# First pass of a two-layer attention kernel: query and output products as seven products of halves, formed inside one strip

## The chip, the cores and the metric

The kernel runs on one core of a Trainium2 chip. The metric is the device time of one execution in microseconds. Of the kernel before, three executions took 3718.24, 3722.89 and 3724.72 us; the median is 3722.89 us. The engines are named as in the profile: PE (TensorE: matrix products; PEld is its weight load), DVE (VectorE), ACT (ScalarE), POOL (GpSimd), SP (SyncE, which here issues the DMAs). Each engine works through its own queue in order. A product lands in one of eight PSUM banks, of 512 float32 columns each, from which DVE or ACT must read it.

## The reference, cut to what matters

The input has 8 images of 256 channels and 64x64 positions, all float32. Layer 0 is an attention with keys and values from a 4x4-strided convolution; layer 1 is a linear attention with a depthwise convolution.

```python
xr = layernorm(conv(x, w_sr, stride 4))              # 16x16 = 256 positions
q  = w_q @ x                                         # 256x256 by 256x4096
k, v = split(w_kv @ xr)
attn = softmax(q_head.T @ k_head * 32**-0.5)         # 8 heads of 32, 256 keys
out  = w_out @ (attn @ v)
x2   = x + gamma_s * out                             # end of layer 0
qkv  = w_qkv @ x2                                    # 768x256 by 256x4096, layer 1
...                                                  # depthwise, linear attention, projection
```

The change touches `w_q @ x`, `gamma_s * (w_out @ ...)` and how the seven products of `w_qkv @ x2` are put together.

## The kernel before, in words

The kernel has three passes. Only the first, the function `first_pass`, is touched. It computes layer 0 and the product `w_qkv @ x2`, and stores `x2`, the q and k planes, k and v to scratch memory for the later passes.

**Tiling.** An image's 4096 positions are cut into 8 strips of 512 columns (`QB`). `strips(b, s)` is a strip in SBUF: 128 partitions, two channel halves, 512 columns. The list `order` runs over image `b`, strip `s` and channel half `c`: 8 x 8 x 2 = 128 iterations, counted by `n`. Each iteration handles four heads of one strip.

**One iteration `n` of the main loop (from L1045), as it stands on PE.**

1. `scores(..., 0, q)` (L795): four products of 32 rows for the keys 0 to 127, side by side in four row groups, into four banks. ACT then turns each bank into `e` (L801, an exponential).
2. `valued` and `counted` for the iteration before: eight products into one bank `av` (L819) and four into one bank `den` (L839). `den` takes the sums `ej` that POOL adds from the two sets of `e` (`joined`, L832).
3. `scores(..., 1, q)`: the same for the keys 128 to 255, with four more `e`.
4. `copied` and `normed` for the iteration before: ACT copies `av` to `att` (L843). DVE turns `den` over (L852), takes the reciprocal (L854), turns it back (L856) and multiplies `att` (L858).
5. Some of the products of `qkv` (L917), the query products of the next iteration, and, in every second iteration, the output products `added`. Where the next image's keys are in preparation (`keys_values`), products `sr` (L707) of 256 columns are put in between: 64 for each image but the first.

`queries` (L780) makes one channel half of a strip's queries as two products of 512 columns; ACT copies the bank (L788). `added` (L873) does the same for the output, and DVE multiplies the bank by `gamma_s` and adds it into the strip in one instruction (L874), after which the strip is stored.

**Seven products.** `qkv` works on a pair of strips (a group `g`) and a pair of output halves. The operand is a 2x2 arrangement of blocks, channel half by strip, and so is the weight. Instead of eight products of a 128x128 weight with 512 columns it makes seven: products 1 to 7 of sums and differences of blocks, whose results DVE adds up (`part`, `whole`, `stage`: L930, L933, L986, L990, L999). Every product has a bank of its own. The differences of strips come from `differences`: three DVE instructions and one on POOL (L888 to L891). The sums of weights come from `combine_weights`. The pairs 1, 2, 0 of a group are spread over four iterations in portions of 7, 4, 7 and 3 products. Of the results, `turned` transposes (L937) and the `stage` copies on ACT (L943) come one iteration later (`late`, run by `catch_up`).

**Banks.** `bank` hands out eight banks in rotation; a bank named as kept (`av`, `den`, `sr`) leaves the rotation until `given_back`. A product waits until the readers of the bank's previous content are done.

**Order.** The program's instructions are put in order for each engine, ahead of time, by a planner with its own estimates of cost; instructions marked with `keep_in_program_order` stay behind all that the program wrote earlier for that engine. In the kernel before, few are marked (the transposes L852 and L937, the weight products of `conv_weights`); PE's order is the planner's.

`conv_weights` (L683) makes 64 blocks of weights for the second pass on DVE, one in each iteration from 17 to 80.

Of the kernel before, what the change touches and what calls it, by code (L numbers as in the profile page):

```python
# [574 lines left out]
def first_pass(ctx: ExitStack, tc: tile.TileContext, a, fine, planes, x2d, kd, vd, wtd):  # L575
# [30 lines left out]

    consts, x_tiles = {}, {}
# [33 lines left out]
    combined = halves.tile([P, 3, 4, P], F32, tag="combined", name="combined")  # L641

    def combine_weights():
        w = consts["wqkv"].rearrange("p c (j r o) -> p c j r o", j=3, r=2)
        a11, a12, a21, a22 = (w[:, c, :, r] for r in range(2) for c in range(2))
        s1, s2, s3, s4 = (combined[:, :, i] for i in range(4))
        nc.vector.tensor_add(s1, a21, a22)
        nc.vector.tensor_sub(s2, s1, a11)
        nc.vector.tensor_sub(s3, a11, a21)
        nc.vector.tensor_sub(s4, a12, s2)  # L650
# [23 lines left out]
    def conv_weights():  # L674
        for j in (2, 3, 0, 1):
            wd = made.tile([P, 16, 6, 16], F32, tag="wd", name=f"wd_{j}", bufs=1)
            nc.sync.dma_start(wd[:, :, :4], a.w_big[:, j].rearrange("p g (n f) -> p g n f", n=4))

            tc.keep_in_program_order(nc.vector.tensor_add(wd[:, :, 4:], wd[:, :, 0:4:2], wd[:, :, 1:4:2]))
            for g in range(16):  # L680
                w = made.tile([P, 6 * 16, D1], F32, tag="wb", name=f"wb_{j}_{g}", bufs=1)
                tc.keep_in_program_order(
                    nc.vector.tensor_tensor(  # L683
                        w,
                        wd[:, g].rearrange("p n f -> p (n f)").unsqueeze(2).to_broadcast([P, 6 * 16, D1]),
                        consts["wsmall"][:, j, g].unsqueeze(1).to_broadcast([P, 6 * 16, D1]),
                        ALU.mult,
                    )
                )
                nc.sync.dma_start(wtd[j][:, g], w.rearrange("p n o -> p (n o)"))  # L690
                yield
# [4 lines left out]
    def keys_values(b):  # L696
# [5 lines left out]
        for f, tap in taps:  # L702
            w = keys.tile([P, 2, C], F32, tag="wsr", name=f"wsr_{b}_{f}", bufs=3)
            nc.sync.dma_start(w, a.w_sr[:, :, tap])
            for ci in range(2):
                for oc in range(2):
                    nc.tensor.matmul(  # L707
# [13 lines left out]
        for ci in range(2):  # L721
            nc.tensor.matmul(mean, mean_w, xr[:, ci], start=(ci == 0), stop=(ci == 1))
# [7 lines left out]
        for kc in range(2):  # L730
            for ci in range(2):
                nc.tensor.matmul(
# [311 lines left out]
    for n in range(n_all + 6):  # L1044
# [28 lines left out]
        for f in products[:3]:  # L1073
            f()
# [795 lines left out]
```

## Time and profile before

| what | value |
|---|---|
| median of three executions | 3722.89 us |
| the profiled execution: its time, its span | 3723.3 us, 3721.5 us |
| granted PE clock, mean | 0.991 |
| PE busy | 3655.3 us (98%) |
| DVE busy | 2050.1 us (55%) |
| ACT busy | 1348.7 us (36%) |
| POOL busy | 1362.7 us (37%) |
| first score product to last `qkv` product | 57.5 us to 1976.4 us |

The page cuts the span into 40 slices of 93 us. PE shows 9 tenths or more in nearly all of them. The first 21 slices are the first pass; the DMA queues are about half busy there and nearly full in the second pass. All times "at" are microseconds from the span's start. In the timeline a row gives the start, the length from the first start to the last end, the engine, the line, the operation, what is written and read, the shape, and how many equal instructions follow each other; in brackets stands the idle time of the engine before it and what ended it. A float32 product shows as two PE records.

### The profile page before, as it was taken

The page shows a single profiled execution, that of the slowest core. Times are in us where ns is not written, and L with a number is a line of the kernel's source. Part 1 is how long each engine was busy: PE and PEld are TensorE (multiplying, and loading weights), DVE is VectorE, ACT ScalarE, POOL GpSimd, SP SyncE. Part 2 cuts the span into 40 slices and gives each one's busy share as a digit, 9 for nine tenths or more (in the row PEclk, how much of TensorE's full clock was granted, in tenths as well). Part 3 has the DMA queues.
Part 4 walks back from the last instruction along what each step waited for, and adds up shares of the span by engine and source line. Part 5 has one row for each costly group of instructions (what it writes and reads, how often), then busy time and mean ns, then how long its engine had stood idle before and what let it go on. Part 6 is the DMA issues. An engine that isn't in the chain of part 4 may idle for free.

```text
span 3721.5 us, 65545 instructions
## 1 busy us (share of the span) xinstructions
PE 3655.3 (98%) x25506; PEld 2021.3 (54%) x25506; DVE 2050.1 (55%) x3159; ACT 1348.7 (36%) x2761; POOL 1362.7 (37%) x1394
## 2 busy tenths in 40 slices
PE   8999999999999999999998999999999999999998
PEld 4443534435334344353336888888888884333333
DVE  1567576675766755746675544444444445445442
ACT  2344354443443534434542222322222223333322
POOL 2434343343443433434443333433334321222222
PEclk9999999999999999999999999999999998999999
DMA  5336456464464553543648999999989968778773
GB/s 180 103 104 188 130 143 179 129 190 145 123 206 120 150 156 106 145 124 96 176 111 234 265 275 273 252 248 263 266 242 261 240 187 234 224 216 238 226 213 102
DMA packets 557071, 693.98 MB, mean 186 GB/s; under 512 B 79952, under 2 KB 416336, under 8 KB 556752
## 3 DMA queue, kind: packets, MB, share of 16 engines
q1 hardware_dynamic: 556752, 689.70, 66.2%
q8 instruction: 203, 3.33, 0.4%
q14 instruction: 116, 0.95, 0.1%
HBM read 415.15 MB, written 274.40 MB: 185 GB/s over the span
## 4 chain that ended last, share of the span: by engine, by line
PE 94%; DMA 2%; DVE 1%; ACT 1%; issue 1%; SPq 1%; POOL 0%; POOLq 0%; ACTq 0%; DVEq 0%
PE qkv L917 16%; PE p L1593 12%; PE cv L1244 9%; PE cv L1248 9%; PE sc L795 7%; PE sums L1294 7%; PE av L819 6%; PE o L873 6%; PE q L780 6%; PE sr L707 6%; PE den L839 3%; PE rep L1579 2%; PE den L1560 1%; PE raw L1277 1%; DMA wsr<-in_w_sr_dram 1%
## 5 line engine op out<-in xcount | busy, mean ns | idle before, releaser
L832 POOL TENSOR_TENSOR ej<-e,e 128x512 f32<-128x512 f32 x512 | 679.2, 1355 | 957.8 <-ACT e L801 957.8
L801 ACT ACTIVATE e<-sc 128x512 f32<-128x512 f32 x1024 | 529.9, 608 | 581.9 <-PE sc L795 581.9
L1244 PE MATMUL cv<-w,c 128*128 128x128 f32 x3072 | 376.9, 280 | 7.3 <-DVE eps L1615 6.2
L1260 DVE TENSOR_TENSOR s<-cv,both 128x512 f32<-128x512 f32 x256 | 176.6, 691 | 374.5 <-PE cv L1244 192.4
L1244 PEld LDWEIGHTS cv<-w,c 128*128 128x128 f32 x3072 | 354.8, 192 | 37.5 <-issue 36.4
L1603 POOL TENSOR_TENSOR y<-z,xs 128x512 f32<-128x512 f32 x128 | 165.7, 1302 | 458.6 <-ACT z L1601 427.0
L1294 PE MATMUL sums<-vq,r 128*32 128x288 f32 x4096 | 308.6, 414 | 0.2 <-issue 0.2
L795 PE MATMUL sc<-q,kk 32*128 32x512 f32 x2048 | 299.6, 639 | 0.0
L917 PE MATMUL qkv<-differences,combined 128*128 128x512 f32 x576 | 291.3, 597 | 0.5 <-POOL differences L890 0.5
L1593 PE MATMUL p<-raw,wp 128*128 128x512 f32 x512 | 246.9, 604 | 5.2 <-ACT z L1601 5.1
L819 PE MATMUL av<-e,vv 128*32 128x512 f32 x2048 | 248.3, 598 | 0.6 <-ACT e L801 0.6
L707 PE MATMUL sr<-x,wsr 128*128 128x256 f32 x1024 | 235.3, 384 | 9.1 <-DMA wsr<-in_w_sr_dram 9.1
L780 PE MATMUL q<-x,wq 128*128 128x512 f32 x512 | 241.9, 594 | 0.0
L1593 PE MATMUL p<-agg,wp 128*128 128x512 f32 x512 | 240.4, 592 | 0.0
L1248 PE MATMUL cv<-c,w 128*128 128x128 f32 x2048 | 239.1, 275 | 0.0
L1248 PEld LDWEIGHTS cv<-c,w 128*128 128x128 f32 x2048 | 234.3, 192 | 0.0
L873 PE MATMUL o<-att,wout 128*128 128x512 f32 x512 | 231.2, 593 | 0.0
L1251 ACT COPY both<-cv 128x512 f32<-128x512 f32 x128 | 74.9, 585 | 429.1 <-PE cv L1244 370.1
L707 PEld LDWEIGHTS sr<-x,wsr 128*128 128x128 f32 x1024 | 195.8, 192 | 63.8 <-issue 26.2
L852 DVE STREAM_TRANSPOSE rden<-den 128x512 f32<-128x512 f32 x128 | 90.9, 710 | 216.7 <-PE den L839 211.8
L788 ACT COPY q<-q 128x512 f32<-128x512 f32 x128 | 75.1, 586 | 371.7 <-PE q L780 371.7
L933 DVE TENSOR_TENSOR whole<-part,qkv 128x512 f32<-128x512 f32 x256 | 172.6, 684 | 67.2 <-ACT part L979 47.3
(143 smaller groups left out, 5277.2 us busy)
## 6 DMA issues: line engine op xcount, KB each, us to landing
vq<-v SPq DMA_DIRECT2D x256, 384.0 KB
planes<-stage SPq DMA_DIRECT2D x128, 578.0 KB
d<-planes SPq DMA_DIRECT2D x128, 578.0 KB
raw<-planes SPq DMA_DIRECT2D x64, 578.0 KB
x<-in_xp_dram SPq DMA_DIRECT2D x64, 512.0 KB
wsr<-in_w_sr_dram SPq DMA_DIRECT2D x128, 256.0 KB
x<-x SPq DMA_DIRECT2D x128, 256.0 KB
k<-turned SPq DMA_DIRECT2D x256, 128.0 KB
```

Of the source, the lines that this page charges most:

```text
L707: nc.tensor.matmul(ps[:, oc], w[:, ci, oc * P : (oc + 1) * P], strips(b, f // 2)[:, ci, f % 2 * NK : (f % 2 + 1) * NK], start=(f == ci == ...
L780: nc.tensor.matmul(ps, consts["wq"][:, ci, c * P : (c + 1) * P], strips(b, s)[:, ci], start=(ci == 0), stop=(ci == 1),)
L795: nc.tensor.matmul(scs[h], kks[b][rows, c, kc * P : (kc + 1) * P], qs[rows], start=True, stop=True)
L801: nc.scalar.activation(e, scs[h], AF.Exp, scale=D0**-0.5)
L819: nc.tensor.matmul(sums["av"][cols], vvs[b][:, kc, c * P + h * D0 : c * P + (h + 1) * D0], es[h], start=(kc == 0), stop=(kc == 1),)
L832: nc.gpsimd.tensor_tensor(e, es0[h], es1[h], ALU.add)
L873: nc.tensor.matmul(ps, consts["wout"][:, c, oc * P : (oc + 1) * P], att[c], start=(c == 0), stop=(c == 1))
L917: nc.tensor.matmul(ps, w, x, start=True, stop=True)
L1244: nc.tensor.matmul(out, x, m, start=(da == 0), stop=(da == 1))
L1248: nc.tensor.matmul(out, m, x, start=(da == 0), stop=(da == 1))
L1294: nc.tensor.matmul(ps[h * D0 : (h + 1) * D0, : 36 * D1].rearrange("p (r n e) -> p r n e", r=3, e=D1), kt[:, par, h, 2 * r + c], vq[:, r : ...
L1593: nc.tensor.matmul(as_block(ps, i // 2), wp[:, i, oc * P : (oc + 1) * P], block(g, i // 2, i % 2, j), start=(i == 0), stop=(i == 3),)
```

## The change

1. **`sevenfold`** is a new function for seven products of a 2x2 arrangement. It makes products 1, 6, 7 and 5 into banks of their own, and then products 2, 4 and 3 *into the banks of 1, 7 and 5*, added to what stands there (`start=False`). So between the two uses of a bank its first content must have been read: product 2 comes after ACT's copy of product 1, product 4 after DVE's sum `u3`, product 3 after the result `c22`. The banks of 1, 7 and 5 are kept until then. `qkv` uses it in place of its own seven.
2. **Queries and output** use it too, within one strip: the blocks are channel half by column half (256 columns, `NK`). A strip's queries are seven products of 256 columns where they were four of 512, and its output likewise. Four differences of blocks are needed for each strip (`turned_over`, 256 columns): on POOL for the queries, on DVE for the output. The partial sums `small1` to `small3` have one buffer each, which the query and the output products share.
3. **Output**: the second operand is added in several instructions: each of the four blocks of the strip gets its bank added by DVE, and three of them a partial sum added by POOL.
4. **`gamma_s`** is multiplied into `w_out` once, at the start; `combine_weights` also makes the weight sums for `w_q` and `w_out`.
5. **Order**: every PE product of the first pass is marked to stay in program order (`pe`). The loop is written anew. With `turn = n % 4`: in turns 2 and 0 the seven `qkv` products stand together; in turn 3 four of them stand before the query products and three behind; turn 1 has the output and the query products, interleaved, and turn 2 has output products after `qkv`. The `sr` products come by a table `taps`.
6. Smaller tiles: `conv_weights` makes its blocks in two halves; `att` has 3 buffers for 4, `whole` 4 for 6, `wsr` 4 for 3.

```diff
@@ combine_weights
-    combined = halves.tile([P, 3, 4, P], F32, tag="combined", name="combined")
+    combined = halves.tile([P, 5, 3, P], F32, tag="combined", name="combined")
...
+        nc.vector.tensor_scalar_mul(consts["wout"], consts["wout"], consts["gam"][:, 0:1])
+        for i, n, w in ((0, 3, consts["wqkv"]), (3, 1, consts["wq"]), (4, 1, consts["wout"])):
...
+            nc.vector.tensor_add(s1, a21, a22)
+            nc.vector.tensor_sub(s2, s1, a11)
+            nc.vector.tensor_sub(a21, a11, a21)
+            nc.vector.tensor_sub(s4, a12, s2)
@@ sevenfold
+        def product(i, w, x, on=None):
+            if on:
+                i = on
+            else:
+                ps[i] = bank(f"{name}_{i}", None if i == 6 else f"{name}_{i}")[:, :width]
+            pe(ps[i], w, x, start=on is None, stop=True, skip_group_check=True)
+            return ps[i]
+        def p1():
+            u[1] = part(1)
+            nc.scalar.copy(u[1], product(1, a11, b11))
+        def p6():
+            u[2] = part(2)
+            nc.vector.tensor_add(u[2], u[1], product(6, s2, t2))
+            done(2)
+        def p7():
+            u[3] = part(3)
+            nc.vector.tensor_add(u[3], u[2], product(7, s3, t3))
+        def p5():
+            c22(u[3], product(5, s1, t1))
+        def p2():
+            c11(product(2, a12, b21, 1))
+            given_back(f"{name}_1")
+        def p4():
+            c21(u[2], product(4, a22, t4, 7))
+            given_back(f"{name}_7")
+            done(4)
+        def p3():
+            c12(u[2], product(3, s4, b22, 5))
+            given_back(f"{name}_5")
+            done(3)
+        return [p1, p6, p7, p5, p2, p4, p3]
@@ turned_over, small
+        sub = lambda o, x, y: nc.gpsimd.tensor_tensor(o, x, y, ALU.subtract) if early else nc.vector.tensor_sub(o, x, y)
+        sub(t1, b12, b11)
+        sub(t3, b22, b12)
+        sub(t2, b22, t1)
+        sub(t4, b21, t2)
+    def small(name):
+        return lambda i: halves.tile([P, NK], F32, tag=f"small{i}", name=f"small_{name}_{i}", bufs=1)
@@ queries: results y11 by ACT, y12, y21, y22 by DVE
-        nc.scalar.copy(qs, ps)
+                lambda ps: nc.scalar.copy(y11, ps),
+                lambda u, ps: nc.vector.tensor_add(y12, u, ps),
+                lambda u, ps: nc.vector.tensor_add(y21, u, ps),
+                lambda u, ps: nc.vector.tensor_add(y22, u, ps),
@@ added
-        nc.vector.scalar_tensor_tensor(
-            xt[:, oc], ps, consts["gam"][:, 0:1], xt[:, oc], ALU.mult, ALU.add
-        )
+                nc.vector.tensor_add(y, y, given[-1])
...
+        def last(u, ps):
+            nc.vector.tensor_add(y22, y22, ps)
+            nc.gpsimd.tensor_tensor(y22, y22, u, ALU.add)
+        def done(i):
+            if i == 2:
+                for y in (y12, y21):
+                    nc.gpsimd.tensor_tensor(y, y, u2[0], ALU.add)
+            else:
+                oc = 1 if i == 4 else 0
+                nc.sync.dma_start(x2d[b][oc * P : (oc + 1) * P, cols], xt[:, oc])
@@ qkv: c11 is a copy on ACT, the fourth partial sum is gone
+                if u is None:
+                    nc.scalar.copy(inside, rows(ps))
...
-            nc.vector.tensor_add(u[4], u[2], ps)
@@ main loop
+    taps = {6: 1, 7: 1, 8: 4, 9: 3, 10: 1, 11: 1, 12: 4, 13: 3, 14: 2, 15: 4}
...
+        asks = n % 2 and n // 2 + 1 < B * NG
+        if asks:
+            query_terms(n // 2 + 1)
...
+        if turn != 1 and n >= 6:
+            b, g = (n - 6) // 16, (n - 6) % 16 // 4
+            pair = qkv(b, g, (1, 2, 0)[(n - 6) % 4])
...
+        run(pair[:4])
+        if turn != 3:
+            run(pair[4:])
+        sometimes(count // 2)
+        if asks:
+            ask = queries(n // 2 + 1)
+        if turn in (1, 2) and 2 <= n <= n_all + 1:
+            S = n // 2 - 1
+            o = added(S // NG, S % NG)
+        run(o[:4])
+        run(ask[:4])
+        run(o[4:])
+        run(ask[4:])
+        if turn == 3:
+            run(pair[4:])
+        if turn == 1 and n > 4:
+            differences(S // NG, S % NG // 2)
+        sometimes(count - count // 2)
```

In the order that the planner makes of the changed kernel, DVE has, in turns 2 and 0, behind the multiplication of `att`: three of the output's four differences (the third, second and fourth; the first is already made), and only then `u2`, `u3` and the results of `qkv`. In turn 1 it has: `u2`, `u3`, block 22 of the output; `u2`, `u3`, block 22 of the queries; blocks 11 and 21 of the output, one difference for the next strip, block 12 of the output, the first of the `differences`, blocks 21 and 12 of the queries. POOL has, in every iteration, the four `ej` first; in turn 1 and turn 2 the three additions of the output stand behind them.

## The prediction

> **What bounds the kernel now.** I read the page first, then a table by stage, then the timeline of each engine over a few iterations, since PE is full on average and only the order of work can tell what a shorter PE is worth.
>
> ```profile
> span 3721.5 us, 65545 instructions
> PE 3655.3 (98%) x25506; PEld 2021.3 (54%) x25506; DVE 2050.1 (55%) x3159; ACT 1348.7 (36%) x2761; POOL 1362.7 (37%) x1394
> ```
>
> ```profile
> 1217.00:1269.20 52.20, 52.20 (x239) 18.89 (x238) 38.47 (x54) 26.23 (x64) 23.59 (x25) 1.00 0.46 129
> 57.45:1976.40 1918.95, 1912.31 (x8601) 811.46 (x8600) 1243.51 (x1785) 844.69 (x2058) 779.32 (x801) 1.00 0.50 139
> ```
>
> The second fence has stretch, length, busy us of PE, PEld, DVE, ACT, POOL, clock, DMA share, GB/s. In the main loop of the first pass (57 to 1976 us) PE is never idle, at full clock. DVE has 35% free, ACT and POOL more. So PE's sum sets the pace, as long as nothing makes PE wait.
>
> Rows of PE:
>
> ```profile
> 1208.36 1.89 PE L760 MATMUL k<-xr,wkv 128*128 128x256 f32 x8
> 1210.08 1.88 PE L780 MATMUL q<-x,wq 128*128 128x512 f32 x4
> 1211.80 3.60 PE L873 MATMUL o<-att,wout 128*128 128x512 f32 x8
> ...
> 1243.62 1.14 PE L795 MATMUL sc<-q,kk 32*128 32x512 f32 x8
> 1244.69 1.92 PE L819 MATMUL av<-e,vv 128*32 128x512 f32 x16
> 1246.43 1.04 PE L839 MATMUL den<-ej,ones_w 128*32 128x512 f32 x8
> 1247.40 1.14 PE L795 MATMUL sc<-q,kk 32*128 32x512 f32 x8
> 1248.47 1.13 PE L917 MATMUL qkv<-differences,wqkv 128*128 128x512 f32 x2
> ...
> 1256.39 1.14 PE L795 MATMUL sc<-q,kk 32*128 32x512 f32 x8
> 1269.17 1.14 PE L795 MATMUL sc<-q,kk 32*128 32x512 f32 x8
> ```
>
> From start to start: two 512-column products 1.72 us (0.86 each), four of 256 columns 1.72 us (0.43 each). Half the columns cost half the time. Four iterations without `sr`, from 1217.05 to 1269.17, take 52.1 us. With t = 0 at an iteration's first score product, PE comes to the products of step 5 at t = 4.85.
>
> DVE, ACT and POOL in the same iteration:
>
> ```profile
> 1247.68 0.72 DVE L852 STREAM_TRANSPOSE rden<-den 128x512 f32<-128x512 f32 x1 [1.72 <-PE den L839]
> 1248.43 0.25 DVE L854 RECIPROCAL one<-rden 128x16 f32<-128x16 f32 x1
> 1248.72 0.71 DVE L856 STREAM_TRANSPOSE rall<-one 128x512 f32<-128x512 f32 x1
> 1249.54 1.57 DVE L858 TENSOR_TENSOR att<-att,rall 128x512 f32<-128x512 f32 x1
> ```
>
> ```profile
> 1249.29 5.40 POOL L832 TENSOR_TENSOR ej<-e,e 128x512 f32<-128x512 f32 x4 [4.16 <-ACT e L801]
> ```
>
> DVE is done with `att` at t = 7.5; POOL adds `ej` from 5.7 to 11.1. The multiplication of `att` takes 1.57 here, but 0.69 where no `ej` is running (1236.16). Two operands in SBUF on DVE and a POOL addition shut each other out. How they take turns shows in the second pass:
>
> ```profile
> 2060.80 1.29 POOL L1220 TENSOR_TENSOR red_raw<-kq 128x512 f32<-128x512 f32 x1 [2.03 <-ACT kq L1227]
> 2062.17 1.09 POOL L1221 TENSOR_TENSOR red_raw<-red_raw 128x256 f32<-128x256 f32 x1
> ```
>
> ```profile
> 2060.90 1.77 DVE L1185 TENSOR_TENSOR c<-d 128x544 f32<-128x544 f32 x1
> 2062.59 1.25 DVE L1186 TENSOR_TENSOR c<-d 128x544 f32<-128x544 f32 x1
> ```
>
> L1185 begins 0.10 after POOL's L1220 and ends 0.58 after L1220's end. L1221, queued meanwhile, ends 0.59 after L1185's end, and L1186, next in DVE's queue, 0.58 after L1221's. They alternate, one whole instruction each.
>
> **The change part by part.** The sum is made against the profiled execution, 3723.3 us (span 3721.5), 0.4 above the median of the three.
>
> *PE work.* A strip's queries: 4 x 0.86 = 3.44 becomes 7 x 0.43 = 3.01; its output the same. 128 x 0.43 = 55 us less, all of it on the bound. In the last product of each bank nothing is added: it takes the same time with `start=False`.
>
> *Other engines, by sums.* DVE loses 96 `u4` (0.677), 96 `c11` (0.684) and 128 L874 (0.751), and gets 64 x 11 sums from a bank of 256 columns (0.417, the row of L724) and 64 x 4 differences (0.42 or more): -227 + 294 + 108 = +175 on 1244 of 1919 us. ACT gets about 54, POOL 64 x 7 additions of 256 columns at about 0.7 (half of `ej`'s 1.3): +314 on 779. None becomes full. The price lies in PE's new waits, which I walk through for the four kinds of iteration (turn = n mod 4). PE keeps program order now, so whatever waits on PE holds all behind it.
>
> *Turns 2 and 0.* Products 1, 6, 7, 5, 2 run from 4.85 to 9.15. Product 4 goes into the bank of product 7, so it needs `u3`. DVE's queue: `att` to 7.5; then three differences with two SBUF operands, in the middle of the `ej`. By the alternation: second `ej` to 8.65, difference to 8.9 (0.58 x 256/544 = 0.28), third `ej` to 10.1, difference 10.4, fourth `ej` 11.6, difference 11.85. `u2` (0.69) to 12.55, `u3` to 13.25. Product 4 starts at 13.3, not 9.15: 4.15 us lost. `c22` is read by 13.95, so product 3 follows at once, ending at 15.0. Turn 0 lasts 15.0 (10.9 without the wait); turn 2 adds the output's 3.0: 18.0 (13.9).
> Here is the one cost that no row shows directly: three DVE operations in a row against `ej`. Its lower end is the uncontended row of 0.42 each: product 4 at 10.0, 0.9 lost instead of 4.15. Upper end 4.15. I take the upper, because the second-pass rows show this very case, two in a row.
> [...]
>
> *Turn 3.* Four `stage` copies stand on ACT ahead of the second `e`, as in the iteration from 1229.83:
>
> ```profile
> 1235.87 2.09 ACT L801 ACTIVATE e<-sc 128x512 f32<-128x512 f32 x4
> 1237.79 0.65 ACT L979 COPY part<-qkv 128x512 f32<-128x512 f32 x1
> ```
>
> The second `e` run from 6.05, and the copy of product 1 ends at 8.6. Product 6's bank waits for the first of those `e`: PE reaches 6.7, not 5.7. Then `u2`, `u3`, `c22` to 10.7, the queries' three sums to 11.95; the queries' product 4 waits to 11.55. Turn 3 ends at 15.0, not 13.9: 1.1 lost.
>
> *Turn 1.* The output's `u2`, `u3` come at 7.5 to 8.4. The queries' `u2` needs the single buffer `small2`, which POOL's two additions of the output still read, and these stand behind the four `ej` (end 11.1): 11.1 + 2 x 0.7 = 12.5. `small3` is free at 13.2, `u3` at 13.65, block 22 at 14.05. PE's product 4 of the queries goes at 13.7, product 3 ends at 14.55, where 10.9 was possible. Next the first score product needs block 12 of the queries, last in DVE's queue behind three output sums, an output difference, one 512-wide difference (0.69) and block 21: 16.9. Turn 1 lasts 16.95: 6.1 lost. [...]
>
> *Sum.* 18.0 + 15.0 + 15.0 + 16.95 = 65.0 against 52.1: +12.9, times 32 = +413 (the 55 saved are in it). In seven images two turns 1 carry three `sr` groups of 1.72 each; one stands in the first wait, and two behind replace the second: 4.1 of 5.2 hidden, -57.
>
> *Start.* Before, four query products filled PE's waits for weights (1.0 us each); now seven products with their sums stand behind the last `sr`: +3 (0 to 10).
>
> *At nothing:* `combine_weights`' additional sums and the scaling run while PE makes `sr`; the halves of `conv_weights` (0.95 becomes two of about 0.5) and 64 more DMA issues (0.3 each on SP) lie in idle time, which is now larger; uncovered 5 and 20 us. Fewer buffers of `att`, `whole`: their last readers end an iteration earlier. The second and third pass are the same.
>
> 3723 + 413 - 57 + 3 = **4082 us**.
>
> **The rivals.**
> *B, the waits are partly there:* the differences slip between the `ej`. Turns 2 and 0 lose 0.9 each: 58.5 per four, +6.4 x 32 = 204 - 57 + 3: 3873. For it: DVE's free 35%. Against: the alternation.
> *C, nothing waits* (the other side): PE stays full and the 55 us are kept: 3723 - 55 + 3 = 3671. It needs `u3` in turns 2 and 0 by t = 9.15 and block 12 of the queries by 10.9; but the chain from `den` (3.8) through `att` alone ends at 7.5, and one difference, `u2`, `u3` already make 9.3.
> *D, worse:* POOL's clearing of `stage` waits for stores of `planes` (before, 9 us after the copy: 1235.5 to 1244.70) ahead of the additions in turn 1. If they land 3 us later than the `ej` end, 31 x 3 = 93: 4175.
>
> **How the numbers follow.** A 0.60 (4082, own range 4010 to 4170), B 0.24 (3870 to 4010), C 0.07, D 0.09. The range 3870 to 4170 leaves out C, most of D and little of B. No change is taken as within 0.2% (7 us), about what measurement can tell: faster 0.07, same 0.01, slower 0.92.
>
> **What would show it.** PE idle of some 350 us or more in the first pass, ended by DVE `part` and `small` and POOL's additions to `x`; the differences at 1.2 to 1.6 us in place of 0.42 where `ej` runs; products of 256 columns at 0.43; four iterations at 65 us; the later passes unchanged in length. Wrong if PE remains above 95% busy in the loop, or if DVE's differences take 0.4 us.

## The result, and the profile after

The changed kernel takes 4290.55 us (median of four executions, 4283.83 to 4292.68), the kernel before 3723.80 on the same chip (3718.24 to 3725.06): a ratio of 1.152, 95% interval 1.1502 to 1.1542. The forecast was 4082 us, its range ended at 4170. The direction was right, the size was not: some 209 us are missing. The profiled execution has a span of 4288.1 us.

The page after: span, busy time, PE in 40 slices, granted clock in 40 slices.

```profile
span 4288.1 us, 68890 instructions
PE 3816.6 (89%) x26274; PEld 2226.1 (52%) x26274; DVE 2366.2 (55%) x3876; ACT 1395.6 (33%) x2921; POOL 1726.2 (40%) x1842
PE   7888887887887887888887889999999999999999
PEclk9999898998998998998998999999999999899999
```

PE is now 7 to 8 tenths busy in the first pass, and full after it: the two later passes have kept their lengths (busy time of the groups `cv` 376.9 and 374.3 us, `sums` 308.6 and 308.3, `p` 246.9 twice). But one line does not fit a kernel that has less PE work: PE's busy time *rose*, from 3655 to 3817 us. The clock row says why; it has sagged to 8 tenths in many slices.

By stretches (stretch, length, busy us of PE, PEld, DVE, ACT, POOL, clock, DMA share, GB/s): the main loop from the first to the last `av` product, in the kernel before and after.

```profile
61.80:1949.60 1887.80, 1881.71 (x8509) 798.91 (x8512) 1217.62 (x1745) 835.14 (x2038) 774.54 (x794) 1.00 0.50 139
```

```profile
60.20:2514.60 2454.40, 2044.09 (x9261) 1001.60 (x9264) 1538.13 (x2445) 880.21 (x2192) 1131.38 (x1231) 0.90 0.39 107
```

The loop is 566.6 us longer, all of the difference. From the trace's records of PE and of the clock: PE's idle time in it went from 6 to 410 us (+404; 407 of it in 145 waits of more than 0.3 us). In 84 stretches of together 468 us the granted clock is one half; PE is busy for 373 us of these, and work that takes 373 us at half speed would have taken 186. So +404 + 186, less the 55 us of work saved, are 535 of the 567; 32 us I cannot assign. Some 24 of them may be this (an estimate): a pair of 512-column products lasts 1.02 us in the rows but the next starts after 0.86, and these 0.16 us are covered except ahead of a wait, so 145 times.

What PE waits for in the first pass (us in total, times, longest):

```profile
PE qkv L608 <- DVE part L817: 240.1, 63, 6.7
PE q L608 <- DVE small_q L817: 76.1, 35, 3.4
PE q L608 <- DVE rden L939: 48.8, 8, 6.1
PE sc L608 <- DVE q L872: 26.3, 23, 2.1
PE qkv L608 <- ACT e L888: 10.4, 14, 0.7
```

The first row is product 4 of `qkv` waiting for `u3` in turns 2 and 0. One of them, turn 2 from 1246.52, on PE:

```profile
1250.30 1.14 PE L608 MATMUL sc<-q,kk 32*128 32x512 f32 x8
1251.37 1.12 PE L608 MATMUL qkv<-x,wqkv 128*128 128x512 f32 x2
...
1254.91 1.02 PE L608 MATMUL qkv<-x,wqkv 128*128 128x512 f32 x2
1260.41 2.07 PE L608 MATMUL qkv<-differences,wqkv 128*128 128x512 f32 x2 [4.48 <-DVE part L817]
1262.28 1.61 PE L608 MATMUL qkv<-x,combined 128*128 128x512 f32 x2
```

on DVE:

```profile
1252.36 1.51 DVE L695 TENSOR_TENSOR wb<-wd,wsmall 128x384 f32<-128x384 f32 x1 [1.97 <-DMA wt<-wb]
1253.80 0.70 DVE L939 STREAM_TRANSPOSE rden<-den 128x512 f32<-128x512 f32 x1
...
1255.64 1.13 DVE L945 TENSOR_TENSOR att<-att,rall 128x512 f32<-128x512 f32 x1
1256.80 1.37 DVE L842 TENSOR_TENSOR terms_o<-att,att 128x256 f32<-128x256 f32 x1
1258.09 0.87 DVE L842 TENSOR_TENSOR terms_o<-att,terms_o 128x256 f32<-128x256 f32 x2
1258.88 0.68 DVE L812 TENSOR_TENSOR part<-part,qkv 128x512 f32<-128x512 f32 x1
1259.67 0.69 DVE L817 TENSOR_TENSOR part<-part,qkv 128x512 f32<-128x512 f32 x1
```

and the granted clock (the third column from the end) in that wait and behind it, and in and behind a wait of turn 0:

```profile
1255.80:1260.40 4.60, 0.13 (x1) 0.00 (x0) 4.38 (x6) 0.59 (x1) 2.09 (x2) 0.96 0.00 0
1260.40:1264.50 4.10, 4.09 (x12) 2.29 (x12) 1.95 (x3) 0.00 (x0) 0.00 (x0) 0.63 0.00 0
```

```profile
1213.48:1217.23 3.75, 0.01 (x1) 0.00 (x0) 3.56 (x4) 0.59 (x1) 2.02 (x2) 0.79 0.63 114
1217.23:1222.50 5.27, 5.27 (x8) 2.83 (x9) 2.54 (x4) 0.00 (x0) 0.00 (x0) 0.50 0.26 52
```

The forecast chain is there: `att`, then the output's differences, then `u2` and `u3`, then product 4, at t = 13.9 (13.3 was forecast). But here the time agrees by chance. The first DVE row is new: a weight block that waited for a store, with the transposition of `den` behind it, so that `att` ends at t = 10.2 and not 7.5; and only the first of the three differences still meets an `ej`. The larger omission is the second row of the last fence: when PE resumes, the clock is at 0.50, and in the wait of turn 2 a product of 0.86 us takes 1.87 (from 1260.41 to 1262.28).

Where no weight block is made, the forecast order and its times both hold. Turn 0 from 2301.41, on DVE, POOL and PE:

```profile
2307.34 1.57 DVE L945 TENSOR_TENSOR att<-att,rall 128x512 f32<-128x512 f32 x1
2308.94 1.37 DVE L842 TENSOR_TENSOR terms_o<-att,att 128x256 f32<-128x256 f32 x1
2310.23 2.88 DVE L842 TENSOR_TENSOR terms_o<-att,terms_o 128x256 f32<-128x256 f32 x2
2313.04 0.67 DVE L812 TENSOR_TENSOR part<-part,qkv 128x512 f32<-128x512 f32 x1
2313.82 0.69 DVE L817 TENSOR_TENSOR part<-part,qkv 128x512 f32<-128x512 f32 x1
```

```profile
2307.09 5.75 POOL L919 TENSOR_TENSOR ej<-e,e 128x512 f32<-128x512 f32 x4 [8.33 <-ACT e L888]
```

```profile
2314.56 1.92 PE L608 MATMUL qkv<-differences,wqkv 128*128 128x512 f32 x2 [3.73 <-DVE part L817]
```

`att` ends at t = 7.5, the differences, among the four `ej`, at 11.7 (forecast 11.85), `u3` at 13.1 (13.25), and product 4 starts at 13.15 (13.3).

### The profile page after: what moved, and what is told of

The parts are those of the page before. It is cut to its first block, busy times and chain, and to the rows that moved or that the text cites. A ratio compares the mean times of both kernels' runs of the same rounds, so it can differ in the third digit from the quotient of the medians.

```text
span 4288.1 us, 68890 instructions
## 1 busy us (share of the span) xinstructions
PE 3816.6 (89%) x26274; PEld 2226.1 (52%) x26274; DVE 2366.2 (55%) x3876; ACT 1395.6 (33%) x2921; POOL 1726.2 (40%) x1842
## 4 chain that ended last, share of the span: by engine, by line
PE 50%; DVE 7%; DMA 3%; POOL 3%; issue 2%; ACT 1%; SPq 1%; DVEq 0%; POOLq 0%; ACTq 0%
PE p L1679 10%; PE cv L1334 8%; PE cv L1330 8%; PE sums L1380 6%; PE qkv L608 4%; PE sc L608 2%; PE av L608 2%; DVE terms_o L842 2%; POOL ej L919 2%; PE sr L608 2%; PE rep L1665 2%; PE o L608 1%; DMA raw<-planes 1%; PE den L1646 1%; PE den L608 1%
## 5 line engine op out<-in xcount | busy, mean ns | idle before, releaser
L919 POOL TENSOR_TENSOR ej<-e,e 128x512 f32<-128x512 f32 x512 | 697.0, 1389 | 877.1 <-ACT e L888 877.1
L608 PE MATMUL qkv<-differences,wqkv 128*128 128x512 f32 x384 | 252.6, 745 | 240.2 <-DVE part L817 240.1
L1330 PE MATMUL cv<-w,c 128*128 128x128 f32 x3072 | 374.3, 279 | 5.1 <-ACT both L1337 3.6
L608 PE MATMUL sc<-q,kk 32*128 32x512 f32 x2048 | 311.3, 674 | 26.3 <-DVE q L872 26.3
L1380 PE MATMUL sums<-vq,r 128*32 128x288 f32 x4096 | 308.3, 413 | 0.5 <-ACT r L1348 0.5
L608 PEld LDWEIGHTS qkv<-differences,wqkv 128*128 128x128 f32 x384 | 76.7, 221 | 359.8 <-DVE part L817 293.5
L1679 PE MATMUL p<-raw,wp 128*128 128x512 f32 x512 | 246.9, 604 | 8.0 <-ACT z L1687 7.8
L608 PE MATMUL sr<-x,wsr 128*128 128x256 f32 x1024 | 245.4, 394 | 7.7 <-DMA wsr<-in_w_sr_dram 7.7
L939 DVE STREAM_TRANSPOSE rden<-den 128x512 f32<-128x512 f32 x128 | 89.9, 703 | 245.2 <-PE den L608 236.2
L1275 POOL COPY c<-d 128x544 f32<-128x544 f32 x64 | 48.3, 756 | 407.9 <-PE cv L1330 372.9
L608 PE MATMUL qkv<-differences,combined 128*128 128x512 f32 x384 | 198.6, 599 | 13.8 <-ACT e L888 10.4
L608 PE MATMUL qkv<-x,wqkv 128*128 128x512 f32 x384 | 207.3, 622 | 0.0
```

The source lines that it names most:

```text
L608: tc.keep_in_program_order(nc.tensor.matmul(*args, **kw))
L919: nc.gpsimd.tensor_tensor(e, es0[h], es1[h], ALU.add)
L939: tc.keep_in_program_order(nc.vector.transpose(turn.rearrange("p n d -> p (n d)"), den))
L1330: nc.tensor.matmul(out, x, m, start=(da == 0), stop=(da == 1))
L1380: nc.tensor.matmul(ps[h * D0 : (h + 1) * D0, : 36 * D1].rearrange("p (r n e) -> p r n e", r=3, e=D1), kt[:, par, h, 2 * r + c], vq[:, r : ...
L1679: nc.tensor.matmul(as_block(ps, i // 2), wp[:, i, oc * P : (oc + 1) * P], block(g, i // 2, i % 2, j), start=(i == 0), stop=(i == 3),)
```

## The experiments

All are measured beside the kernel before. A theory, T: the loss is PE's waits, which come from the order of work on DVE and POOL, *and* a half clock that follows each wait of some microseconds. Mean lengths of the turns below are from one `av` group to the next, in iterations without `sr` (another choice of these iterations moves them by up to 1 us, in all runs much alike); before 12.8, 12.8, 14.2, 12.8 us for turns 0, 1, 2, 3, in the changed kernel 16.6, 19.1, 21.4, 16.5.

### Is the half clock worth anything by itself?

```diff
+    def fill(k):
+        for i in range(k):
+            spare = psum.tile([P, 512], F32, tag=f"bank{turns[0]}", name="spare")
+            pe(spare, ident, consts["wqkv"][:, 0, :QB], start=True, stop=True)
...
-            run(pair[4:])
+            run(pair[4:5])
+            if pair:
+                fill(4)
+            run(pair[5:])
```

The first run also has fills in turns 1 and 3.

> Products that nobody reads (the weights of qkv, 512 columns, into the bank that the next product takes anyway) are put into PE's waits: four behind product 2 of qkv in turns 2 and 0, two behind product 2 of the queries in turn 1, one in turn 3, one at the end of turn 1. The output is unchanged. Theory (a half clock follows each of PE's waits): in the main loop of the changed kernel PE ran 471 us at half clock, 375 us of it busy, so 188 us of the time are the clock's. The fills lie in the waits of 4 us, PE has more to do by 320 products and yet is faster: 4110 to 4170 us, granted clock above 0.97. Rival (the half clock costs nothing of its own, the products stretched would have waited anyway): 4290 us or up to 30 more, since the fills of turns 1 and 3 are not all covered; granted clock may rise, the time does not fall.

Measured: 4268.19 us, ratio 1.1465 (1.1446 to 1.1485), clock 0.981. Neither number. Turn 0 fell to 14.9 and turn 2 to 19.4 us, but turn 1 grew to 22.0: its fills delayed product 4 of the queries, and the score products behind waited 2.6 us on the mean in place of 1.1. So the fills of turns 2 and 0 alone:

> Only the four fills behind product 2 of qkv in turns 2 and 0 (3.44 us of 512-column products that nobody reads, in waits of about 4 us); the other fills are left out. In the run with all fills, turn 0 went from 16.6 to 14.9 us and turn 2 from 21.4 to 19.4, while turn 1 grew from 19.1 to 22.0. Theory (the half clock costs some 1.7 to 2 us in each turn 2 and 0, and the fills in turn 1 were too long): turn 1 stays at 19.1, so 64 x 1.7 to 2 = 110 to 130 us less: 4160 to 4185 us. Rival (what turns 2 and 0 gain, turn 1 waits for in any case, since it waits for DVE's and POOL's queues): turn 1 grows without fills too, 4250 to 4290 us.

Measured: 4182.09 us, ratio 1.1235 (1.1216 to 1.1253), clock 0.977, as the theory said. PE has 256 products of 512 columns more to do and the kernel is 108 us faster. A wait of turn 2, filled:

```profile
1203.01 1.02 PE L608 MATMUL qkv<-x,wqkv 128*128 128x512 f32 x2
1203.87 4.57 PE L608 MATMUL spare<-wqkv,ident 128*128 128x512 f32 x8
1208.53 1.13 PE L608 MATMUL qkv<-differences,wqkv 128*128 128x512 f32 x2
1209.49 1.02 PE L608 MATMUL qkv<-x,combined 128*128 128x512 f32 x2
```

Product 4 comes no earlier, but products 4 and 3 are 0.96 us apart and not 1.87. PE's half-speed loss in the loop fell from 186 to 57 us; what is left belongs to the waits of turns 1 and 3. Turn 0 now takes 14.9 us on the mean; the forecast, made without a half clock, had 15.0.

### What makes the waits of turns 2 and 0?

First without the output's differences:

```diff
+    still = halves.tile([P, 4, NK], F32, tag="still", name="still")
+    nc.vector.memset(still, 0.01)
+    fixed = tuple(still[:, i] for i in range(4))
...
-        t = turned_over(f"terms_o_{b}_{s}", b11, b12, b21, b22, False)
+        t = fixed
```

> The four differences of the output on DVE are left out for every strip; its products 6, 7, 5 and 4 take a constant tile instead, so the values of the output are not the reference's. The query differences keep one buffer. Theory (product 4 of qkv waits for sums that stand behind these differences, and the clock halves after it): the waits behind product 2 in turns 2 and 0, 239 us in the trace of the changed kernel, and the half clock behind some 60 of them, 60 x 3.4 / 2 = 102 us, go: 3930 to 3970 us; DVE's sum u3 comes at t = 8.9, before PE asks for it. Rival (product 4 waits because it is added in a bank, whatever stands in DVE's queue): only DVE's own time goes, 256 x 0.42 = 107 us at most: 4180 us or more, with waits behind product 2 of 3 us and more.

Measured: 3960.07 us, ratio 1.0637 (1.0619 to 1.0655): 330 us for differences that would take 107 us with nothing in the way (all 256 together take 256 us in the changed kernel's trace). Turn 0 there, DVE:

```profile
1688.07 1.57 DVE L948 TENSOR_TENSOR att<-att,rall 128x512 f32<-128x512 f32 x1
1689.72 0.69 DVE L812 TENSOR_TENSOR part<-part,qkv 128x512 f32<-128x512 f32 x1
1690.52 0.69 DVE L817 TENSOR_TENSOR part<-part,qkv 128x512 f32<-128x512 f32 x1
```

`u3` is done at 1691.2, as PE reaches product 4 (1691.40), and PE goes on without a wait; turn 0 takes 11.1 us in such iterations. The addition in the bank costs nothing here: products 4 and 3 start 0.86 us apart (1691.40 and 1692.26), like the others. Of the waits for `part` 43 us are left, 40 of them in the four images in which weight blocks are made. Next the same work, put behind:

```diff
+            else:
+                tc.keep_in_program_order(nc.vector.tensor_sub(o, x, y))
...
+        if turn in (0, 2) and 2 <= n <= n_all:
+            out_terms((n // 2 - 1) // NG, (n // 2 - 1) % NG)
```

`out_terms` makes the four differences; it is called behind `qkv`.

> The same work as the changed kernel, but the four differences of the output are written and kept behind the sums of qkv in DVE's queue, in turns 0 and 2. Theory: product 4 of qkv no longer waits in either turn. In turn 0 the differences then fall into the next iteration's start, where DVE is idle; in turn 2 the output's product 6 waits for the third difference, some 2 us: 4290 - 341 + 30 x 2 to 4 (with the clock behind it) = 4010 to 4070 us. Rival (the place does not matter, the differences lose the same time to the ej wherever they stand): within 60 us of 4290.

Measured: 4043.79 us, ratio 1.0853 (1.0833 to 1.0872). Turn 0 takes 11.3 us on the mean. In turn 2 the output's products wait for the differences (25 times, 2.8 us each): the wait is moved and smaller, as expected. So 247 us of the loss are the *place* of 256 small DVE instructions.

Then the banks and PE's order:

```diff
+            if own:
+                on = None
+                ps[i] = bank(f"{name}_{i}")[:, :width]
...
+        def own4():
+            c21(u[3], product(4, a22, t4))
```

> qkv's products 2, 4 and 3 get banks of their own again, with the two additional DVE sums (block 11 and the fourth partial sum); wsr has 3 buffers for 4. DVE's order otherwise as in the changed kernel, with the output's differences in front. Theory (DVE's queue is late, the addition in the bank only decides which product meets it): products 4 and 3 start without waiting, but the banks of products 6 and 7 are wanted by the next score products or the output's, and u2 and u3 read them only at t = 12.5 and 13.2: PE waits 2.4 us there in place of 4: 4130 to 4290 us, with waits in front of sc and o. Rival (adding in the bank is what makes PE wait): the waits of turns 2 and 0 and their half clocks go, 4290 - 341 = 3950 us or less.

Measured: 4282.95 us, ratio 1.1499 (1.148 to 1.1519). The total speaks against the rival's 3950 us, but it does not test the size that the theory gave, because of the side edit: with three buffers the weights of `sr` come late in turn 0 (14 waits, 97 us). In turns 0 without `sr` the theory's mechanism shows; PE runs all seven products and then stands in the score products, which come in two parts:

```profile
1925.05 1.02 PE L608 MATMUL qkv<-x,combined 128*128 128x512 f32 x2
1926.00 1.13 PE L608 MATMUL sc<-q,kk 32*128 32x512 f32 x4
1927.30 1.91 PE L608 MATMUL sc<-q,kk 32*128 32x512 f32 x4 [0.17 <-DVE part L815]
1929.47 1.92 PE L608 MATMUL av<-e,vv 128*32 128x512 f32 x16 [0.26 <-DVE part L843]
```

The score groups take 3.3 us where 1.07 is usual, and turn 0 13.2 us: some 2.3 us lost in place of 4. In turn 2 the outputs wait instead (61 us, 28 times, for `small_o`).

```diff
-        tc.keep_in_program_order(nc.tensor.matmul(*args, **kw))
+        nc.tensor.matmul(*args, **kw)
```

> PE's products of the first pass are no longer marked to stay in program order; the planner puts them in order, as in the kernel before. Nothing else changes. Theory (PE is held by a product that waits while others could go): the planner puts other products into a part of the waits, and the half clock goes with those: 3950 to 4200 us. Rival (the chains of sums are the bound whatever the order, since the kept banks leave no product that could go): 4240 to 4300 us.

Measured: 4290.50 us, ratio 1.1523 (1.1504 to 1.1543): no difference. The planner moved the output of turn 1 into turn 2 (turn 1 14.0 us, turn 2 25.5), and PE's wait for `part` L817 stayed at 234.7 us. PE's fixed order is not the cause.

### What do the output and the queries cost?

```diff
-        return lambda i: halves.tile([P, NK], F32, tag=f"small{i}", name=f"small_{name}_{i}", bufs=1)
+        return lambda i: halves.tile([P, NK], F32, tag=f"small{i}" if i == 1 else f"small{name[0]}{i}", name=f"small_{name}_{i}", bufs=1)
```

> small2 and small3 of the output and of the queries are separate buffers (wsr has 3 buffers instead of 4 to make the room). Theory: the wait of PE behind product 2 of the queries in turn 1 (24 times, 60 us in all, in the changed kernel's trace) is DVE's wait for POOL's two additions that read small2, so it goes, with some 25 us of half clock behind it: 4200 to 4230 us. Rival (the queries' sums come late because DVE's queue is long): 4270 to 4300 us.

Measured: 4258.67 us, ratio 1.1429 (1.141 to 1.1448): 32 us, half of the least that the theory gave. Its waits on PE:

```profile
PE qkv L608 <- DVE part L817: 237.1, 63, 5.6
PE sc L608 <- DVE q L872: 53.8, 26, 4.0
PE q L608 <- DVE rden L939: 28.4, 8, 3.6
PE sr L608 <- DMA wsr<-in_w_sr_dram: 20.4, 14, 2.7
PE q L608 <- DVE small_q L817: 18.9, 13, 3.3
```

The wait for `small_q` did go (76 to 19 us), so the shared buffers, which POOL's two additions still read, were its cause. But the next one grew, the score products' wait for block 12 of the queries, 26 to 54 us: that chain ends last in turn 1, whatever stands ahead of it. The three `sr` buffers cost another 20.

Each part undone, in one run each. The output:

```diff
+        def half(oc):
+            ps = bank(f"o_{b}_{s}_{oc}")
+            for c in range(2):
+                pe(ps, consts["wout"][:, c, oc * P : (oc + 1) * P], both[c], start=(c == 0), stop=(c == 1))
+            nc.vector.tensor_add(xt[:, oc], xt[:, oc], ps)
...
+        return [lambda: half(0), lambda: half(1)]
```

> The changed kernel with its output undone: four products of 512 columns in banks of their own and one DVE sum each, as in the kernel before (the scale stays in the weights). Queries and qkv as changed. Theory (the output's differences in DVE's queue make the waits of turns 2 and 0, its additions on POOL those of turn 1): like the run without the differences (3960), 27 us more for PE, and the waits behind product 2 of the queries in turn 1 (60 us and some 25 us of half clock) gone: 3880 to 3920 us. Rival (each of the three uses of seven products costs its own share): two thirds of the loss stay, 4100 us.

Measured: 3829.57 us, ratio 1.0277 (1.0258 to 1.0296), 50 us below the theory's lowest. PE's wait for `part` is down to 22 us and that for `small_q` to 14.

The queries, in the same way:

```diff
+        def half(c):
+            ps = bank(f"q_{n}_{c}")
+            for ci in range(2):
+                pe(ps, consts["wq"][:, ci, c * P : (c + 1) * P], strips(b, s)[:, ci], start=(ci == 0), stop=(ci == 1))
...
+            nc.scalar.copy(q[2 * n + c], ps)
```

> The changed kernel with its queries undone: four products of 512 columns and copies on ACT, as before; output and qkv as changed. Theory: the waits of turns 2 and 0 (239 us, and the half clock behind them) stay; the waits of query products in turns 1 and 3 (60 + 49 + 15 us) and in front of the score products go, with some 40 us of half clock, and PE has 27 us more: 4120 to 4170 us. Rival (turn 1 is bound by the output's chain through POOL and the differences, with or without queries): 4250 us or more.

Measured: 4161.31 us, ratio 1.1172 (1.1153 to 1.1192), as the theory said; PE's wait for `part` stays, at 228 us. Of the 567 us the output as seven products carries 461, the queries 129. The two do not have to add up to the whole, since they share turn 1.

### Is the saved work a gain at all?

The sum counted 55 us of PE work as a gain. The kernel before with the queries alone as seven products (27.5 us of it), each with a bank of its own:

```diff
+        nc.scalar.copy(u[0], product(1, w[:, 0, 0], b11))
+        nc.vector.tensor_add(u[1], u[0], product(6, s2, t2))
+        nc.vector.tensor_add(u[2], u[1], product(7, s3, t3))
+        nc.vector.tensor_add(q0[:, :NK], u[0], product(2, w[:, 1, 0], b21))
+        p5 = product(5, s1, t1)
...
+        if n % 2 and n + 1 < n_all:
+            q.update(queries(n // 2 + 1, terms))
```

> The kernel before with one part of the change alone: the queries as seven products of 256 columns, each in a bank of its own, differences on POOL, sums on DVE; PE's order is the planner's; the weight products of conv_weights in halves and whole with 5 buffers, to make the room. Output and qkv as before. If PE stays full, 64 x 0.43 = 27.5 us less: 3696 us. If the chain of sums holds PE as in the changed kernel (2 to 3 us in every second iteration, with a half clock behind some): 3850 to 3950 us.

Measured: 3826.42 us, ratio 1.0283 (1.0257 to 1.0309). Neither number. Of the 91.5 us that its loop is longer, 43 are waits and 18 half clock, and 27.5 should be saved: 58 are something else. The planner had broken groups of products up:

```profile
566.68 0.70 PE L811 MATMUL q<-terms,combined_q 128*128 128x256 f32 x2
568.95 5.33 PE L829 MATMUL sc<-q,kk 32*128 32x512 f32 x18 [1.58 <-DVE q L820]
...
582.25 1.04 PE L853 MATMUL av<-e,vv 128*32 128x512 f32 x2
585.17 1.09 PE L829 MATMUL sc<-q,kk 32*128 32x512 f32 x2 [1.88 <-DVE rden L886]
```

Score products run four at a time in four row groups, 1.07 us for a set of four; alone, one took 1.02 (from 585.17 to 586.19). So PE was put in program order, and the queries' sums behind what is written earlier:

```diff
+    def pe(*args, **kw):
+        tc.keep_in_program_order(nc.tensor.matmul(*args, **kw))
...
+        def add(*args):
+            tc.keep_in_program_order(nc.vector.tensor_add(*args))
...
         for f in products[3:]:
             f()
+        if n % 2 and n + 1 < n_all:
+            second()
```

> The kernel before with the queries alone as seven products, as in the run that took 3826 us, but PE's products marked to stay in program order, the last three query products behind the rest of qkv, the queries' DVE sums marked to stay behind what is written earlier, and the halves of the weight products one in each iteration. In the run at 3826 us the planner's order of PE had broken 41 of the 250 groups of score products and 12 of the 128 groups of av apart, and PE waited 43 us more. Theory (the seven products themselves gain 27.5 us, and it was order and waits that cost 130): with groups whole and sums in time 3690 to 3715 us, below the kernel before. Rival (the chain of sums holds PE in any order): 3760 us or more.

Measured: 3858.94 us, ratio 1.0357 (1.0341 to 1.0372). The groups are whole, but PE waits 107 us more than before, for the queries' last sum and for weight loads, with 22 us of half clock behind: 107 + 22 - 27.5 = 101, and the loop is 100 us longer; nothing is left over, which fits the broken groups as the 58 us, though this run changed other places too. Three more runs moved what the trace before each showed as late. First the place of the last three query products and of the `sr` groups:

```diff
-        taps = 2 if filled and 6 <= at < 10 else 0
+        slots = (3 if at < 12 else 2) if filled and at >= 6 else 0
...
-        for f in products[3:]:
+        for f in products[3:5]:
             f()
         if n % 2 and n + 1 < n_all:
             second()
+        for f in products[5:]:
+            f()
```

> As the run that took 3859 us (the kernel before with the queries as seven products in banks of their own, PE in program order), with the two waits that its trace showed moved: the last three query products stand ahead of qkv's products 5 and 3 instead of behind them, so that the queries' last sum is not the last thing before the score products (49 us of PE's waits there); and the sr products come one group at a time, three places in an iteration from 6 to 11, instead of two by two, so that their weights are loaded in time (49 us). Theory (idle time and half clock are all that stood against the 27.5 us of PE work saved: 107 + 22 - 27.5 = 101 of the 100 us that its loop was longer): with those waits below 20 us the time falls below the kernel before, 3695 to 3720 us. Rival (each wait removed only uncovers the next one on DVE): 3740 us or more.

Measured: 3780.05 us, ratio 1.0155 (1.0141 to 1.0169). The waits for the queries' sums went from 54.5 to 3.6 us; 37 us for `sr` weights stayed, and 20 us came at the second pass's start, where the weight products now ended late.

```diff
+            while len(ws) <= f + (2 if b else 0) and len(ws) < len(taps):
+                fetch()
...
+        if n > 4 and n % 2 == 0:
+            next(weights, None)
```

> As the run that took 3780 us (the kernel before with the queries as seven products), with its last waits moved: the sr weights are loaded two groups ahead, so that their loads do not stand behind the stores of x on SP (in that run PE waited 37 us for them, with some 15 us of half clock behind); and the weight products of conv_weights, which there lasted until the first pass ended and held the second pass up by 20 us, end after about 90 iterations. Theory (25 us of PE work saved count as soon as no wait stands against them): 3695 to 3715 us, below the kernel before. Rival (the saved work is given back in any case, since an iteration with seven query products is bound by DVE): 3725 us or more.

Measured: 3810.98 us, ratio 1.0238 (1.0217 to 1.0259), the wrong way: the second weight product of an iteration waits for the store of the first, and the transposition of `den` behind it on DVE made PE wait 36.5 us.

```diff
-        slots = (3 if at < 12 else 2) if filled and at >= 6 else 0
+        slots = (3 if at < 12 and at != 8 else 2) if filled and at >= 6 else 0
...
-        if n > 4 and n % 2 == 0:
+        if n > 4 and n % 4 == 2:
```

> As the run that took 3811 us, with the second weight product of conv_weights only in turn 2 (in the run before, the one at the end of turn 0 waited for the store of the one before it, and DVE's transposition of den in turn 1 stood behind it: 15 waits of 2.4 us on PE), and one sr group fewer in the iteration whose weights came late (8 waits of 3.3 us). In the run at 3811 us the image behind the weight products, iterations 96 to 111, took 242.0 us against 242.6 in the kernel before, one late load in it. Theory: without these waits the time falls below the kernel before, 3695 to 3718 us. Rival (an iteration with seven query products is bound by DVE in any order): 3725 us or more.

Measured: 3761.27 us, ratio 1.0109 (1.0092 to 1.0126). No version came below the kernel before: all four theories missed, and the rivals' totals came. But the open question has its answer where no wait stands: four iterations with two strips' queries, without `sr` and weight blocks, PE at full clock (the same columns as above):

```profile
1752.15:1803.49 51.34, 51.34 (x247) 21.13 (x246) 41.34 (x66) 24.25 (x61) 29.43 (x31) 1.00 0.42 107
```

51.34 us against the 52.12 of the kernel before: 0.78 less, forecast 2 x 0.43 = 0.86. The saved work is a gain, and DVE is no bound there, which was the rival's reason. Whole images show it too. From `av` to `av` of every sixteenth iteration, images 2, 3, 4 and 7 took 242.9, 244.9, 242.8 and 201.3 us in this run, and 245.2, 245.1, 245.1 and 205.7 in the kernel before. The gain is lost in the other images: the first is 12.5 us longer, images 1 and 5 6 each, image 6 2. So the loop as a whole is 18 us longer than before (30 more of waits, 9 of half clock, 27.5 saved; 7 not assigned), and the span 17 us more outside the loop; I did not follow these up.

## Why the prediction was wrong, point by point

**The step that failed is the sum:** all products in it go by their full-clock rows (0.86 and 0.43 us), also behind the waits that the same sum forecasts. It had no term for the clock, which measured 186 us in the loop. When PE was kept busy in turns 2 and 0, this loss fell to 57 us and the kernel became 108 us faster. With the 186 us, the forecast would have been 4268. The hint was in the kernel before, in its first 60 us:

```profile
37.86 5.38 PE L707 MATMUL sr<-x,wsr 128*128 128x256 f32 x16 [2.23 <-DMA wsr<-in_w_sr_dram]
```

```profile
39.00:42.40 3.40, 3.40 (x9) 2.69 (x8) 0.15 (x1) 0.00 (x0) 0.00 (x0) 0.50 1.06 396
```

Eight products of 0.43, 3.4 us, took 5.4 behind a wait of 2.2. In the changed kernel's loop a half clock followed 76 of 79 waits above 3 us, and 8 of 22 between 1.5 and 2.5 us (how they are counted stands in the last section).

- **Waits, total:** the waits forecast turn by turn are 266 + 35 + 195 - 57 = 439 us, 404 measured: 35 too many. But the sum holds only 413 + 55 - 57 = 411 us of them. It adds up the new turns product by product (65.0) and takes off the measured 52.1, where the same adding up gives 51.2 for the kernel before (4 x 4.85 + 21 x 0.86 + 4 x 3.44). That lost 28 us. The two errors nearly cancel; that 411 is close to 404 is luck. Of the 209 us that the forecast lacks, 186 are thus the clock and 28 this, with the 32 us not assigned; the 35 us of waits and 3 us of start that did not come go the other way.
- **Turns 2 and 0:** 64 x 4.15 = 266 us forecast, 240 measured (63 waits). The upper bound was the right choice: the differences took 1243 and 1154 ns on the mean (forecast 1.2 to 1.6 us; 417 ns for an uncontended sum of the same size), since they alternate with `ej`, as in turn 0 from 2301.41: of the three that stand behind `att`, in the changed kernel's trace, the 150 that lay beside an `ej` for more than half of their time took 1.40 us on the mean, the 42 that met none 0.42. The sums `u2` and `u3` of `qkv`, which read a bank, took 0.69 us beside an `ej` and 0.68 without one. One row of the prediction was misread: at 1236.16 an `ej` does start (1236.58), 0.42 us into the multiplication of `att`, which had begun first and took its 0.69 us all the same. Rival B falls.
- **Turn 1:** 195 - 57 = 138 us forecast, about 135 measured, but the agreement is partly luck: 49 us of it are eight waits of product 5 for the bank of `den`, whose transposition the planner had put behind `small_q`. I did not see that. The forecast order of the two others (`small2` first, then block 12) is right, and the run with separate buffers shows it.
- **Turn 3:** 35 us forecast, 28 measured.
- **PE work:** 256-column products are 0.43 us apart at full clock, as forecast (in the changed kernel from 667.71 to 668.14 and to 668.57).
- **"At nothing":** wrong for the halves of `conv_weights`. The second half waits for the store of the first (162 us in 56 waits on DVE), with `den`'s transposition behind it. In the changed kernel images 2 to 4, which carry weight blocks, took 321 us each, images 5 and 6, nearly without, 310 (before: 245 and 243). In the run with the output undone it was 266, 266 and 274 us against 251 and 247, so there the blocks may be the larger part of the 106 us that are left. No run of the changed kernel takes the halves back, so this share is not shown by an experiment.
- **Start:** no loss; the first `av` came at 60.2 us, before at 61.8.
- **Rivals:** C falls, the waits came. D's total was the nearest, for a wrong reason: PE's waits are explained without POOL's clearing of `stage`.

## What to carry to other kernels

In this kernel a wait on PE cost more than its length: 186 us of half clock came with 79 waits of more than 3 us and a few shorter ones, some 2 us for each long wait, and four products that nobody reads in each turn 2 and 0 brought the 186 down to 57. Look up in the trace what follows such a wait and price it in, or give PE something to do. A short instruction put ahead of a chain costs what the chain's reader loses, not what it takes: 256 differences, 0.42 us each with nothing in the way, cost 247 us by their place alone. When a new loop is added up by hand, add up the old one in the same way. A saving in work on a full engine is only worth what the new chains leave of it, and the first thing to look for is which sum ends last before the next stage.

## What the hardware showed that was not expected

In the changed kernel's loop the granted clock fell to exactly 0.50, for stretches of 3.41, 6.83 or (rarely) 10.24 us: 33, 49 and 2 of the 84. A wait counts as followed by such a stretch if one begins between 1 us after the wait's start and 3 us behind its end; often it begins before PE resumes (in 58 of the 79 waits above 3 us). Counted so in that trace, of PE's waits of 0.3 to 1.5 us 1 in 44 was followed by such a stretch, of those from 1.5 to 2.5 us 8 in 22, of those above 3 us 76 in 79 (one stretch is counted with two waits, the one in 44 among them). None lies between 2.5 and 3.
